# Cross-attention scores in a decoder layer: two one-pass matmuls over 128 rows instead of one fp32 matmul over 64, and the weighing of values in two halves

## The chip, the cores and the metric

The kernel runs on one core of a Trainium2 chip, as one program. The metric is device time in microseconds (us) from start to end of an execution; lower is better. TensorE is called PE here, its weight loads PEld, VectorE DVE, ScalarE ACT, GpSimd POOL, SyncE SP.

## The reference, cut to what matters

A decoder layer on x of shape (4, 512, 512): self-attention with 16 heads of 128 channels, cross-attention with 8 heads, and a feed-forward part whose weights are rounded to three values. The change lies in the cross-attention.

```python
x = x + attn(layernorm(x), Wq, bq, Wk, bk, Wv, bv, Wo, bo)   # 16 heads, attention between channels
x = x + xattn(layernorm(x), ctx, ctx, gamma)
x = x + ffn(layernorm(x), w1, w3, w2)                        # silu(x w1') * (x w3'), then w2'; hidden size 1365

def xattn(q, k, v, gamma):            # k and v are both ctx
    B, Dq, Lq = q.shape               # 4, 512, 512
    qh = q.reshape(B, 8, 64, 512)     # a head is 64 whole rows
    kh = k.reshape(B, 8, 64, 512)
    vh = v.reshape(B, 8, 64, 512)
    qk = einsum('bhdq,bhdl->bhql', qh, kh) / sqrt(64)
    sm = softmax(qk, axis=-1)
    ret = einsum('bhql,bhdl->bhdq', sm, vh)
    return gamma * ret.reshape(B, 512, 512)
```

So each head's scores are a 512 x 512 matrix that sums over only 64 rows, and the result sums over 512 keys into 64 rows.

## The kernel before, in words

**Two kinds of matmul.** An fp32 matmul leaves two records in the profile, a matmul on operands of type F32R one ("one-pass"). F32R holds fewer digits, so the kernel cuts an operand into a high part, rounded to F32R, and a remainder (`h` and `l`), and `products` (lines L311 to L336) adds up matmuls of such parts: L318 for the high parts, L319 for the remainders, L330 for a third part. Names with `_1h` are its results, as in `pu_1h`; `uh`, `ul`, `ud` are parts of a left operand, `ol` and `xl` of another, `fxh` and `fxl` of the feed-forward input.

**Order of the work.** Image b=0's self-attention comes first, with weights as they arrive; it leaves cut weights in DRAM. Then a loop over b = 1, 2, 3 runs the self-attention of image b on PE, four groups of heads each (`u`, `y`, `m`, scores `sc`, output `po`). Beside it two generators are stepped: `side` does `row_norms(b - 1)` and then `cross(b - 1)`, `quant` rounds the feed-forward weights. `products` calls `tick()` three times per pair of its results; the class `Side` (L163) takes as many steps of its generator at each tick as keep it in proportion: `CROSS_STEPS + NORM_STEPS` steps over `TICKS + 6` ticks. The last image's cross-attention runs in the same way beside the feed-forward matmuls `h` (L1005) and `y` (L1032) of the first images; in that part DVE makes `gf`, `gl` and the row statistics of the next feed-forward input. Within these ticks the program is put in order by a scheduler from the order of issue and from what is ready; each engine then works strictly in its order.

**The cross-attention.** A block c is 128 rows: two heads of 64. There are four blocks per image, 16 in all.

- `row_norms` (L638) takes mean and 1/std of each row of the self-attention's result `acc`, stores them to DRAM (`norm_a`, L648, issued on POOL) and loads them back in another layout (`norms`, L650, on POOL): one column pair per block. `settle` (L569) is a small DVE instruction on the loaded tile.
- `prepare(c)` loads the 128 rows of x (`cx`), normalizes them on DVE (`qs`, L117), loads `keys`, and transposes these on PE into `vals`. All of its loads are issued on POOL.
- `softmax_rows(c, m)` (L673) takes 128 queries of both heads: one fp32 matmul per head over 64 rows (`xs`, L680), the two heads in different rows of the array, then maxima on DVE (L686), exponentials on ACT (L692), the scaling by 1/sum on DVE (L704).
- `transpose_rows(c, m)` transposes the weights on PE (`xp`, L123) and DVE and ACT copy them to `pt`.
- `weigh_values(c)` (L717) runs after four such steps: eight fp32 matmuls of 128 x 64 by 128 x 512 (`xo`, L724), two heads in different columns of the array, then gamma and the addition of x on DVE (L731) and the store of `x_c`.

The steps are woven: transposition follows two softmax steps behind, the values of c are weighed during the first step of c+1, and block c+1 is prepared after step m = 2 of block c. Pools have three buffers for `cx`, two for `qs`, `keys`, `vals` and `pt`, four for `p`. POOL also issues the loads and stores of the rounded weights and adds the bias to `acc`; the SP queue brings the attention's weights.

## Time and profile before

| | |
|---|---|
| median of 3 runs | 1184.07 us (1180.95 to 1184.69) |
| the profiled execution | 1185.08 us, its span 1183.3 us |
| granted clock of PE, mean | 0.999 |
| `xs` L680, 256 records | 72.0 us busy on PE |
| `xo` L724, 256 records | 61.7 us busy on PE |
| `xp` L123, 512 records | 65.7 us busy on PE |
| maxima L686, 128 on DVE | 83.9 us |
| exponentials L692, 128 on ACT | 87.1 us |
| DMA | 254.11 MB, mean 215 GB/s |

The span is from the first to the last instruction; the time of an execution has some 2 us around it. Busy times of PE overlap, since matmuls are pipelined: the mean duration of a record is longer than the distance from one start to the next, and only the latter says what a matmul takes of the span. Records are counted, not calls: an fp32 matmul leaves two. PE's busy time by stage, from windows of the trace: 65.39 of the first 75 us, 195.31 of the 200 us to 275, 199.04 of the 200 to 475, 224.69 of the 225 to 700, and 478.49 of the 483 after it. The chain that ended last runs over PE for 80% of the span.

In the rows of the page an operation is given as out<-in by the program's names, then partitions x elements; "x256" is the number of records. A timeline row is start, duration, engine, line, operation. Windows list for each stretch its length, busy time of PE, PEld, DVE, ACT and POOL, the granted clock (1.00 is full), the DMA engines' busy share and GB/s.

### The profile page before, as it was taken

How to read it: one execution, taken by the hardware profiler on the slowest of the kernel's cores; microseconds unless marked ns; L12 is line 12 of the kernel's file. 1: busy time of each engine (PE TensorE's matmuls, PEld its weight loads, DVE VectorE, ACT ScalarE, POOL GpSimd, SP SyncE). 2: the span in 40 equal slices, each digit the busy share in tenths (PEclk: the TensorE clock that was granted, in tenths of full speed). 3: DMA queues.
4: the chain of work that ended last, by engine and by line, in shares of the span. 5: the costliest groups of instructions: out<-in, count | busy, mean ns of one | idle time of the engine just before them, and what ended most of it. 6: DMA issues, size and time to landing. Idle time of an engine off the chain costs nothing.

```text
span 1183.3 us, 16165 instructions
## 1 busy us (share of the span) xinstructions
PE 1162.9 (98%) x5278; PEld 821.8 (69%) x5278; DVE 805.7 (68%) x1806; ACT 452.0 (38%) x948; POOL 247.6 (21%) x419
## 2 busy tenths in 40 slices
PE   7999999999999999999999999999999999999998
PEld 3476674777767667777676677777667767768886
DVE  5879678978687966767587758586866745535232
ACT  2221223434434433434254424343454746634020
POOL 3545343431121223001111320011011000000000
PEclk9999999999999999999999999999999999999999
DMA  9898996786788659776876597587772220011201
GB/s 311 275 354 314 329 362 221 269 308 230 234 272 299 188 209 330 252 245 231 284 272 234 185 346 255 175 323 257 292 244 83 72 72 10 18 63 45 71 1 54
DMA packets 140030, 254.11 MB, mean 215 GB/s; under 512 B 16164, under 2 KB 47188, under 8 KB 139946
## 3 DMA queue, kind: packets, MB, share of 16 engines
q1 hardware_dynamic: 112266, 164.93, 41.4%
q0 software_dynamic: 27680, 88.16, 20.7%
q8 instruction: 42, 0.69, 0.2%
q14 instruction: 42, 0.34, 0.1%
HBM read 190.09 MB, written 62.93 MB: 214 GB/s over the span
## 4 chain that ended last, share of the span: by engine, by line
PE 80%; DMA 7%; DVE 6%; issue 3%; POOL 1%; ACT 1%; SPq 0%; DVEq 0%; POOLq 0%; ACTq 0%
PE h L1005 14%; PE y L1032 7%; PE xs L680 6%; PE xo L724 5%; PE xp L123 4%; PE sc L488 4%; PE po L525 4%; PE pg L409 2%; PE py_3h L318 1%; PE pu_1d L330 1%; PE py_3h L319 1%; PE py_1h L318 1%; DMA v_raw<-in_wv_dram 1%; PE pu_3d L330 1%; PE py_3d L330 1%
## 5 line engine op out<-in xcount | busy, mean ns | idle before, releaser
L1005 PE MATMUL h<-fxh,t 128*128 128x512 f32 (+1 forms) x352 | 139.8, 397 | 0.0
L692 ACT ACTIVATE p<-xs,xnmax 128x512 f32<-128x512 f32 x128 | 87.1, 688 | 135.7 <-PE xp L123 117.8
L1005 PE MATMUL h<-fxl,t 128*128 128x512 f32 (+1 forms) x352 | 137.4, 390 | 0.0
L686 DVE TENSOR_REDUCE xnmax<-xs 128x1 f32<-128x512 f32 x128 | 83.9, 682 | 18.1 <-PE xs L680 18.1
L1005 PEld LDWEIGHTS h<-fxh,t 128*128 128x128 f32 (+1 forms) x352 | 65.0, 185 | 18.4 <-issue 1.9
L1005 PEld LDWEIGHTS h<-fxl,t 128*128 128x128 f32 (+1 forms) x352 | 65.0, 185 | 14.6 <-issue 0.2
L680 PE MATMUL xs<-keys,qs 64*128 64x512 f32 x256 | 72.0, 640 | 0.0
L1032 PE MATMUL y<-t,gh 128*128 128x512 f32 (+1 forms) x176 | 69.6, 396 | 0.0
L1032 PE MATMUL y<-t,gl 128*128 128x512 f32 (+1 forms) x176 | 68.8, 391 | 0.0
L123 PE MATMUL xp<-ident,p 128*128 128x128 f32 x512 | 65.7, 272 | 0.0
L123 PEld LDWEIGHTS xp<-ident,p 128*128 128x128 f32 x512 | 59.0, 140 | 9.5 <-issue 2.3
L1016 DVE SCALAR_TENSOR_TENSOR gf<-h,scales_w,sl 128x512 f32<-128x512 f32 (+1 forms) x44 | 32.8, 746 | 46.1 <-PE h L1005 37.9
L724 PE MATMUL xo<-pt,vals 128*64 128x512 f32 x256 | 61.7, 599 | 0.9 <-ACT pt L126 0.9
L126 ACT COPY pt<-xp 128x512 f32<-128x512 f32 x96 | 53.5, 595 | 17.9 <-PE xp L123 17.9
L704 DVE TENSOR_SCALAR p<-p,xrden 128x512 f32<-128x512 f32 x128 | 57.5, 492 | 3.4
L525 PE MATMUL po<-m,eT 128*128 128x512 f32 x128 | 58.8, 601 | 0.1
L352 PE MATMUL pm<-u,v_raw 128*128 128x512 f32 x128 | 55.6, 592 | 0.0
L623 POOL DMA_DIRECT2D t_w<-tern_w x43 | 28.8, 672 | 119.9 <-DVE tern_w L616 47.9
L1014 ACT ACTIVATE sl<-h,scales_w 128x512 f32<-128x512 f32 (+1 forms) x44 | 30.1, 689 | 59.1 <-PE h L1005 58.9
L135 POOL CAST gh<-gf 128x512 fp32r<-128x512 f32 (+1 forms) x24 | 14.8, 617 | 177.0 <-DVE gf L1016 156.3
L527 DVE SCALAR_TENSOR_TENSOR acc<-po,acc 128x512 f32<-128x512 f32 x64 | 41.6, 681 | 7.5 <-PE po L525 7.4
L488 PEld LDWEIGHTS sc<-y,q 128*128 128x128 f32 x384 | 44.0, 192 | 2.5 <-issue 2.3
(299 smaller groups left out, 2667.7 us busy)
## 6 DMA issues: line engine op xcount, KB each, us to landing
oh<-kept_oh SPq DMA_DIRECT2D x48, 256.0 KB, 4.6
ol<-kept_ol SPq DMA_DIRECT2D x48, 256.0 KB, 4.9
kh<-kept_kh SPq DMA_DIRECT2D x48, 256.0 KB, 4.8
kl<-kept_kl SPq DMA_DIRECT2D x48, 256.0 KB, 5.2
vh<-kept_vh SPq DMA_DIRECT2D x48, 256.0 KB, 5.7
vl<-kept_vl SPq DMA_DIRECT2D x48, 256.0 KB, 6.1
q<-kept_q SPq DMA_DIRECT2D x48, 256.0 KB, 5.5
od<-kept_od SPq DMA_DIRECT2D x44, 256.0 KB, 5.9
```

Source lines behind the costliest of these rows:

```text
L123: nc.tensor.transpose(pt[:, ts(k, P)], src[:, ts(k, P)], ident)
L126: nc.scalar.copy(dst, pv)
L352: nc.tensor.matmul(p, lhsT=lhs(k)[:, ts(i, P)], rhs=rhs(k), start=(k == 0), stop=(k == 3))
L488: nc.tensor.matmul(sc[:, ts(g, DH)], lhsT=w[k][:, ts(g, DH)], rhs=ys[k][:, ts(g, DH)], start=(k == 0), stop=(k == KC - 1),)
L525: nc.tensor.matmul(po, lhsT=eT[:, g, :], rhs=ms[g], start=True, stop=True)
L680: nc.tensor.matmul(sc, lhsT=qs[rows, ts(m, P)], rhs=keys[rows, :], start=True, stop=True)
L686: nc.vector.reduce_max(nmax[:, j : j + 1], scs[j], axis=AX.X)
L692: nc.scalar.activation(p, scs[j], AF.Exp, bias=nmax[:, j : j + 1], scale=xscale, accum_out=den[:, j : j + 1],)
L704: nc.vector.tensor_scalar(ps[j], ps[j], rden[:, j : j + 1], None, ALU.mult)
L724: nc.tensor.matmul(po[rows, :], lhsT=vals[:, l, rows], rhs=pt[j][:, l, :], start=(l == 0), stop=(l == NC - 1),)
L1005: nc.tensor.matmul(ph[:r, :], lhsT=t[:, block(i, k)], rhs=fxT[j][:, k, :], start=(k == 0 and j == 0), stop=(k == KC - 1 and j == 1),)
L1032: nc.tensor.matmul(py, lhsT=g[i][j][:r, ts(c, P)], rhs=t2[:r, i, :], start=(i == 0 and j == 0), stop=(i == NHC - 1 and j == 1),)
```

## The change

**Scores.** Each head gets a left operand of 128 rows: the normalized queries' high part in rows 0 to 63 and their remainder in rows 64 to 127. The keys' high part stands in both halves of a second tile (`kh`), their remainder in both halves of a third (`kl`). Two one-pass matmuls, [qh; ql] with [kh; kh] and with [kl; kl], add up in one PSUM bank. To get this, `fetch(c)` loads each head's x rows and key rows twice, one copy above the other, in 64-row transfers on POOL; `split(c)` then issues per head, in this order, a normalization in place on ACT, a copy to F32R on ACT, a subtraction on DVE for the lower half, a copy of the keys on ACT, and their subtraction on DVE. The tiles of a head have two buffers, for the two heads of a block.

**Norms.** They are stored as -mean/std and 1/std and loaded twice, once into each half of the partitions, one column pair per head.

**Values.** `weigh_values(c, h)` runs for each two transposed steps, on 256 queries, so `pt` tiles are half as wide, and twice as many groups of matmuls `xo` and of additions run. The rows of x for the addition are loaded once per block at h == 0. `keys` and `vals` have one buffer and are prepared later, `cx` has one.

**Steps.** `CROSS_STEPS` goes from 40 to 49: preparation is three steps (values and fetch after m = 2, split after m = 3), and weighing comes twice per block. A small tile (`gate`) gets four buffers.

```diff
@@ -216,7 +216,7 @@
     def gate_of(src):
 
 
-        gate = small.tile([P, 3], F32, tag="gate", name="gate")
+        gate = small.tile([P, 3], F32, tag="gate", bufs=4, name="gate")
         for i, f in enumerate((H_OF / S, -1.0)):
             nc.vector.tensor_scalar(gate[:, i : i + 1], src[:, 0:1], f, f, ALU.max, ALU.min)
         nc.vector.tensor_tensor(gate[:, 2:3], gate[:, 1:2], ident[:, P - 1 :], ALU.add)
@@ -631,8 +631,9 @@
 
 
     xscale = 1.0 / math.sqrt(XD)
-    CROSS_STEPS = NC * (2 * NC + 2)
+    CROSS_STEPS = 3 * NC * NC + 1
     NORM_STEPS = 2 * NG + 3
+    HALF = T // 2
     norms = {}
 
     def row_norms(b, accs):
@@ -644,42 +645,75 @@
             yield
             moments(mv[:, g, :], accs[g], f"c_{b}_{g}")
         rstd = rstd_of(mv, f"c_{b}")
-        nc.vector.tensor_copy(mv[:, :, 1:2].rearrange("p c s -> p (c s)"), rstd)
+        mean, var = (mv[:, :, i : i + 1].rearrange("p c s -> p (c s)") for i in range(2))
+        nc.vector.scalar_tensor_tensor(mean, mean, -1.0, rstd, ALU.mult, ALU.mult)
+        nc.vector.tensor_copy(var, rstd)
         nc.gpsimd.dma_start(norm_a[b].rearrange("(p g) s -> p g s", g=NG), mv)
-        norms[b] = small.tile([P, NC, 2], F32, tag="norms", bufs=2, name=f"norms_{b}")
-        nc.gpsimd.dma_start(norms[b], norm_a[b].rearrange("(c p) s -> p c s", p=P))
+        norms[b] = small.tile([P, 2 * NC, 2], F32, tag="norms", bufs=2, name=f"norms_{b}")
+        for half in (slice(0, XD), slice(XD, P)):
+            nc.gpsimd.dma_start(norms[b][half], norm_a[b].rearrange("(n p) s -> p n s", p=XD))
         for _ in range(3):
             yield
 
     def cross(b, cx, cin, cpp, cpt):
+
 
 
         def load(dst, src):
             nc.gpsimd.dma_start(dst, src)
             return dst
 
-        def prepare(c):
-
-            xc = load(cx.tile([P, D], F32, tag="x", name=f"cx_{b}_{c}"), x_a[b][ts(c, P), :])
-            qs = cin.tile([P, D], F32, tag="qs", name=f"qs_{b}_{c}")
-            normalize(qs, xc, norms[b][:, c, 0:1], norms[b][:, c, 1:2])
-            keys = load(
-                cin.tile([P, T], F32, tag="keys", name=f"keys_{b}_{c}"), kv[b][ts(c, P), :]
+        def twice(tile, rows):
+            for half in (slice(0, XD), slice(XD, P)):
+                load(tile[half, :], rows)
+            return tile
+
+        def heads_of(c):
+            return [slice(c * P + j * XD, c * P + (j + 1) * XD) for j in range(2)]
+
+        def fetch(c):
+
+            raw[c] = [
+                [
+                    twice(cin.tile([P, T], F32, tag=f"{n}d", bufs=2, name=f"{n}d_{b}_{c}_{j}"), src[r, :])
+                    for n, src in (("x", x_a[b]), ("k", kv[b]))
+                ]
+                for j, r in enumerate(heads_of(c))
+            ]
+
+        def split(c):
+            halves[c] = []
+            for j, (xd, kd) in enumerate(raw.pop(c)):
+                n = 2 * c + j
+                nc.scalar.activation(
+                    xd, xd, AF.Identity, bias=norms[b][:, n, 0:1], scale=norms[b][:, n, 1:2]
+                )
+                q = cin.tile([P, T], F32R, tag="qs", bufs=2, name=f"qs_{b}_{c}_{j}")
+                nc.scalar.copy(q, xd)
+                low = slice(XD, P)
+                nc.vector.tensor_tensor(q[low, :], xd[low, :], q[low, :].bitcast(F32), ALU.subtract)
+                kh = cin.tile([P, T], F32R, tag="kh", bufs=2, name=f"kh_{b}_{c}_{j}")
+                nc.scalar.copy(kh, kd)
+                kl = cin.tile([P, T], F32R, tag="kl", bufs=2, name=f"kl_{b}_{c}_{j}")
+                nc.vector.tensor_tensor(kl, kd, kh.bitcast(F32), ALU.subtract)
+                halves[c].append((q, kh, kl))
+
+        def fetch_keys(c):
+            keys[c] = load(
+                cin.tile([P, T], F32, tag="keys", bufs=1, name=f"keys_{b}_{c}"), kv[b][ts(c, P), :]
             )
-            vals = cin.tile([P, NC, P], F32, tag="vals", name=f"vals_{b}_{c}")
-            transpose_blocks(vals, keys, f"vt_{b}_{c}", c % 2)
-            return xc, qs, keys, vals
+
+        def values(c):
+            vals[c] = cin.tile([P, NC, P], F32, tag="vals", bufs=1, name=f"vals_{b}_{c}")
+            transpose_blocks(vals[c], keys.pop(c), f"vt_{b}_{c}", c % 2)
 
         def softmax_rows(c, m):
 
-            _, qs, keys, _ = inputs[c]
             scs = []
-            for j in range(2):
+            for j, (q, kh, kl) in enumerate(halves[c]):
                 sc = bank(f"xs_{b}_{c}_{m}_{j}")
-                rows = slice(j * XD, (j + 1) * XD)
-                nc.tensor.matmul(
-                    sc, lhsT=qs[rows, ts(m, P)], rhs=keys[rows, :], start=True, stop=True
-                )
+                nc.tensor.matmul(sc, lhsT=q[:, ts(m, P)], rhs=kh, start=True, stop=False)
+                nc.tensor.matmul(sc, lhsT=q[:, ts(m, P)], rhs=kl, start=False, stop=True)
                 scs.append(sc)
             nmax = small.tile([P, 2], F32, tag="xnmax", name=f"xnmax_{b}_{c}_{m}")
             for j in range(2):
@@ -705,58 +739,72 @@
             return ps
 
         def transpose_rows(c, m, ps):
-            if m == 0:
-                pts[c] = [
-                    cpt.tile([P, NC, T], F32, tag="pt", name=f"pt_{b}_{c}_{j}") for j in range(2)
+            h = m // 2
+            if m % 2 == 0:
+                pts[c, h] = [
+                    cpt.tile([P, NC, HALF], F32, tag="pt", name=f"pt_{b}_{c}_{h}_{j}")
+                    for j in range(2)
                 ]
             for j in range(2):
                 transpose_blocks(
-                    pts[c][j][:, :, ts(m, P)], ps[j], f"xp_{b}_{c}_{m}_{j}", j or m % 2
+                    pts[c, h][j][:, :, ts(m % 2, P)], ps[j], f"xp_{b}_{c}_{m}_{j}", j or m % 2
                 )
 
-        def weigh_values(c):
-            xc, _, _, vals = inputs.pop(c)
-            pt = pts.pop(c)
-            po = bank(f"xo_{b}_{c}")
+        def weigh_values(c, h):
+
+            if h == 0:
+                xcs[c] = load(cx.tile([P, D], F32, tag="x", name=f"cx_{b}_{c}"), x_a[b][ts(c, P), :])
+            pt = pts.pop((c, h))
+            po = bank(f"xo_{b}_{c}_{h}")[:, :HALF]
             for l in range(NC):
                 for j in range(2):
                     rows = slice(j * XD, (j + 1) * XD)
                     nc.tensor.matmul(
                         po[rows, :],
-                        lhsT=vals[:, l, rows],
+                        lhsT=vals[c][:, l, rows],
                         rhs=pt[j][:, l, :],
                         start=(l == 0),
                         stop=(l == NC - 1),
                     )
+            xc = xcs[c][:, ts(h, HALF)]
             nc.vector.scalar_tensor_tensor(xc, po, gam, xc, ALU.mult, ALU.add)
-            load(x_c[b][ts(c, P), :], xc)
-
-        inputs, pts, rows = {}, {}, {}
+            if h == 1:
+                load(x_c[b][ts(c, P), :], xcs.pop(c))
+
+        raw, halves, keys, vals, pts, rows, xcs = {}, {}, {}, {}, {}, {}, {}
+        fetch(0)
+        fetch_keys(0)
         settle(norms[b][:, 0, :])
-        inputs[0] = prepare(0)
+        yield
+        split(0)
         yield
         order = [(c, m) for c in range(NC) for m in range(NC)]
         due = None
-        for i in range(len(order) + 2):
+        for i in range(len(order) + 3):
             if i < len(order):
                 c, m = order[i]
                 rows[c, m] = softmax_rows(c, m)
                 yield
             if due is not None:
-                weigh_values(due)
+                weigh_values(*due)
                 due = None
                 yield
-            if i < len(order) and m == 2 and c + 1 < NC:
-                inputs[c + 1] = prepare(c + 1)
+            if i < len(order):
+                if m == 2:
+                    values(c)
+                    if c + 1 < NC:
+                        fetch(c + 1)
+                        fetch_keys(c + 1)
+                    yield
+                if m == 3 and c + 1 < NC:
+                    split(c + 1)
+                    yield
+            if 2 <= i < len(order) + 2:
+                tc_, tm = order[i - 2]
+                transpose_rows(tc_, tm, rows.pop((tc_, tm)))
                 yield
-            if i >= 2:
-                c, m = order[i - 2]
-                transpose_rows(c, m, rows.pop((c, m)))
-                yield
-                if m == NC - 1:
-                    due = c
-        weigh_values(due)
-        yield
+                if tm % 2:
+                    due = tc_, tm // 2
 
 
     TICKS = HG * 3 * 6
@@ -891,7 +939,7 @@
     quant = Side(quantize(), QUANTIZE_STEPS, (B - 1) * TICKS)
     cpool = [
         cpools.enter_context(tc.tile_pool(name=n, bufs=k, side="right"))
-        for n, k in (("c_x", 3), ("c_in", 2), ("c_p", 4), ("c_pt", 2))
+        for n, k in (("c_x", 1), ("c_in", 2), ("c_p", 4), ("c_pt", 2))
     ]
     wpools = ExitStack()
     wp, stp = (
```

## The prediction

> **What bounds the kernel now.** I read the page's busy shares first, then TensorE's timeline around the score matmuls, then the places where TensorE stands still, and last the queues that would have to deliver the new operands. In the first fence the reader is to see that TensorE (PE) is busy for nearly the whole span. In the second, that this is not padding: one-pass matmuls over 128 rows follow each other every 0.23 us, and the gaps open only at `xs` (scores) and `xo` (weighed values).
>
> ```profile
> span 1183.3 us, 16165 instructions
> PE 1162.9 (98%) x5278; PEld 821.8 (69%) x5278; DVE 805.7 (68%) x1806; ACT 452.0 (38%) x948; POOL 247.6 (21%) x419
> ```
>
> ```profile
> 704.39 0.39 PE L319 MATMUL pu_1h<-ol,xl 128*128 128x512 f32 x1
> 704.71 1.13 PE L680 MATMUL xs<-keys,qs 64*128 64x512 f32 x4
> 705.76 0.50 PE L318 MATMUL pu_1h<-oh,xh 128*128 128x512 f32 x1
> 706.10 0.39 PE L319 MATMUL pu_1h<-ol,xl 128*128 128x512 f32 x1
> 706.33 0.40 PE L318 MATMUL pu_1h<-oh,xh 128*128 128x512 f32 x1
> ...
> 308.03 0.39 PE L319 MATMUL pu_2h<-ol,xl 128*128 128x512 f32 x1
> 308.35 3.65 PE L724 MATMUL xo<-pt,vals 128*64 128x512 f32 x16
> 311.93 0.50 PE L318 MATMUL pu_2h<-oh,xh 128*128 128x512 f32 x1
> 312.27 0.40 PE L319 MATMUL pu_2h<-ol,xl 128*128 128x512 f32 x1
> 312.50 0.39 PE L318 MATMUL pu_2h<-oh,xh 128*128 128x512 f32 x1
> ```
>
> So from about 245 us to the end what is saved on PE is saved in full, and any time for which PE waits is lost in full.
>
> **What is saved at the scores.** Starts count, since durations overlap. The step into an `xs` pair is 0.32 us (704.39 to 704.71), the pair takes 1.05, the step after it 0.34, and then steps are 0.23 again. 0.32 + 1.05 + 0.34 less two ordinary steps is 1.25 us for one pair of heads. The other pairs in the timeline repeat it. The changed kernel runs four one-pass matmuls over 128 rows, the shape of `pu_1h`: 4 x 0.227 = 0.91, with no odd step around them. There are 64 pairs (256 records, two for one fp32 matmul, two heads): 64 x 0.34 = 21.8 us less.
>
> A rule of the Trainium skill speaks against this. "TensorE: Matmul & The Clock Gate", section "Measured speedup vs the span model", says that tiles packed into the array cost one matmul's duration plus about 4 ns for each further tile. By it the two heads, packed by rows, would take two records of 0.43 us and hardly more, 0.86, and four one-pass matmuls at 0.91 would be 0.05 dearer: +3 us in all instead of -21.8. The row decides: 1.25 us with its surroundings, every time. What I pay less for is entering and leaving the packed form, not passes.
>
> **What the halved values cost.** `xo` is packed too, by columns: 0.32 + 3.58 + 0.34 - 0.46 = 3.78 us for 16 records in 8 simultaneous pairs. With e for the end of a packed block and s for a step, 2s + e = 1.05 (`xs`) and 8s + e = 3.58 give s = 0.42, e = 0.21. A half keeps the eight steps at half the columns: 8 x 0.21 + 0.21 + 0.20 (odd steps around it) = 2.1; two are 4.2 against 3.78, so +0.41 x 16 = +6.6 us. No row shows a packed matmul of 256 columns. Lower bound: +0.35 x 16 = +5.6 (only the second entry and exit). Upper: the weight loads of the two tiles, 137 ns each in the next fence, no longer fit beneath a step of 0.21 and run one after the other, s = 0.27: 8 x 0.06 x 32 = +15 more. I take +6.6, as in `sc` 128-column fp32 records with loads of 192 ns still start about 0.11 apart (249.56 to 253.04 for 32), so loads overlap. PE alone: -21.8 + 6.6 = -15.2 us.
>
> **What ScalarE, VectorE and POOL get.**
>
> ```profile
> L187 DVE TENSOR_TENSOR ul<-u,uh x48: 671/683/693, 222.1 to 832.0; 128x512 fp32r<-128x512 f32 x48
> L186 ACT ACTIVATE uh<-u 128x512 fp32r<-128x512 f32 x48 | 30.3, 632 | 39.5 <-DVE u L340 38.8 <-DMA acc<-in_x_dram 0.7
> L117 DVE TENSOR_SCALAR qs<-cx,norms x16: 530/538/548, 244.9 to 972.1; 128x512 f32<-128x512 f32 x16
> L724 PEld LDWEIGHTS xo<-pt,vals x256: 132/137/137, 308.3 to 1062.5; 128*64 128x64 f32 x128
> ```
>
> Per block of keys (16 in all) ACT gets two normalizations and four copies: 96 x 0.63 = 60 us, 38% becomes 43%. DVE gets four subtractions, 64 x 0.683 = 44, loses 16 x 0.538 = 8.6, and splits one 0.75 us addition into two of some 0.45 (between 0.28 for 128 columns and 0.75 for 512: +2): +37 us, 68% becomes 71%, and near 79% in the image loop. POOL issues 128 more half-height loads at 0.54 us (69 us) and four more loads of the norms at 0.76; the bytes are 128 x 128 KB = 17 MB on 254. All this lies beside PE, which is the bound; uncovered it costs only where PE finds an operand unready. The transfers have a whole block (about 45 us) for landings of about 5 us. The SP queue, which brings the weights, keeps its order.
>
> **Where a new wait comes.** Queries, key halves and remainders have two buffers for two heads, so those of block c+1 can't be written until the last `xs` of c is read. From the order in which the changed program's instructions stand: in the image loop PE has 8 to 10 us of other matmuls in between; at 0 to 1 DVE has two maxima (1.36), one sum, two `ul` and two `ud` (3.4), and the four subtractions (2.7), with a small one 7.7 us against PE's 9.9. That fits. In the feed-forward part at block 0 to 1 PE has 8.6 us (32 `h` matmuls and 12 transposes), but DVE stands at two maxima 1.4, scalings of `p` 2.0, `fxl`, `gf`, `gl` 2.1, four row statistics of 0.66 with aggregates 3.0, subtractions and small ones 1.9 before the first remainder is done: 10.4, a wait of 1.6, and some 0.9 more for the second head: +2.5 us. Behind it on PE's queue stand the `y` matmuls.
>
> The other place is the first `xs` of an image. The fence shows the norms' way through DRAM for the first one.
>
> ```profile
> 224.72 0.55 POOL L648 DMA_DIRECT2D norm_a<-mv_c  x1 [1.68 <-DVE mv_c L647]
> 231.40 0.76 POOL L650 DMA_DIRECT2D norms<-norm_a  x1 [6.13 <-DMA norm_a<-mv_c]
> ...
> 243.20 0.16 DVE L573 TENSOR_TENSOR norms<-norms,one 128x1 f32<-128x1 f32 x1
> ...
> 247.06 0.40 PE L319 MATMUL pm_0h<-ul,vl 128*128 128x512 f32 x1
> ...
> 255.05 1.13 PE L680 MATMUL xs<-keys,qs 64*128 64x512 f32 x4
> ```
>
> Before, `xs` comes at 255.05, long after the norms. In the changed order it stands right behind that `pm_0h`, at 247.3, while on DVE the two instructions that finish the norms have moved behind the `y` sums (which end near 235.2). So the store goes out at 236.3, the two loads stand behind it and behind three additions of `acc` on POOL; with the store's 6.4 us they go at 242.7 and 243.5, and with the load's 4.1 us the second lands at 247.6. Then ACT (two normalizations, a copy) and DVE (a piece's sum, two `m` sums, a subtraction) need some 2.7 us: 250.3, a wait of 3.0. Behind ACT's waiting instruction are the copies of `pm_0t`, behind DVE's settling of the norms the `m` sums. The second image's norms go out at 450 as before and fit by 0.7 us; the third has the same order.
>
> The second rule: "DMA: Bandwidth & Descriptors", section "Anatomy of one DMA — SWDGE (gpsimd) path", gives a transfer about 2.0 us of fixed cost. By it the second load would land at 244.2 and PE would wait for nothing. Here the rows read 6.4 and 4.1, so I take the wait. Such a wait can also cost clock:
>
> ```profile
> 71.70:74.90 3.20, 0.46 (x3) 0.06 (x1) 1.62 (x5) 2.90 (x10) 2.06 (x4) 1.00 1.07 395
> 75.00:78.30 3.30, 3.30 (x8) 2.58 (x9) 2.56 (x7) 1.82 (x4) 2.23 (x4) 0.50 1.04 399
> 162.40:165.00 2.60, 0.39 (x3) 0.04 (x1) 1.61 (x5) 1.59 (x9) 1.82 (x4) 1.00 1.05 407
> 165.00:168.00 3.00, 3.00 (x13) 2.46 (x14) 2.96 (x9) 1.96 (x4) 2.21 (x5) 1.00 1.07 399
> ```
>
> After PE stood idle to 74.84 the granted clock was 0.50 for about 3.4 us (1.7 us lost); after the shorter pause at 162 it stayed 1.00. A wait of 3.0 lies between: I count +4.0 for wait and clock (bounds 0 and +6.7).
>
> **Sum.** -21.8 + 6.6 + 2.5 + 4.0 = -8.7 us. The profiled execution took 1185.08 (span 1183.3 and 1.8 around it), so 1176.4; it stands 1.0 over the median of 1184.07: about 1175.5.
>
> **Rivals.** (B) No new wait: the queues absorb both. Then -15.2: 1169. For it: ACT has room and DVE waits for no transfer in the image loop. Against: the norms' two landings are measured. (C) Halved values expose their weight loads: +15 on the sum, 1191, or 1184 with no wait. For it: 137 ns twice is more than 0.21. Against: the tiles' loads start together, and `sc`. (D) The other side: the halves come late at every block, at the first `xs` of all 16 groups. For it: single-height buffering, DVE near 79%, and DVE itself waits (31 times for exponentials, 37.6 us in all), while ACT and DVE serve strictly in order. At 2 us a group +32 takes the place of the 6.5: 1184.07 - 15.2 + 32 = 1201. It decides from 1.0 us a group, where the saving is gone. Against: PE's 8 to 10 us of other work. (E) That the change doesn't do what it says is unlikely: the order shows 256 score matmuls over 128 rows in place of 128 over 64.
>
> **Numbers.** 0.3% (3.6 us: 1180.5 to 1187.6) is about what a measurement can tell from no change. The likeliest case 0.55 (its own range 1169 to 1182), B 0.15, C 0.10, D 0.20. Faster: 0.50 + 0.15 + 0.01 = 0.66; same: 0.05 + 0.04 + 0.04 = 0.13; slower 0.21. The range reaches from B's lower edge, 1167, into D, to 1194.
>
> **What would show it.** Right: `xs` steps of 0.23 us with the neighbours at 0.23 too; `xo` blocks of about 1.9 us, 32 of them; PE idle for 2 to 5 us before the first `xs` near 247, waiting for DVE `qs`; a wait of 2 to 3 us in the feed-forward part; other matmuls as before. Wrong: `xo` steps of 0.27; waits for `kl` or `qs` before every first `xs`; a DVE wait for staged weight pieces; PE below full clock away from 250 us.

## The result, and the profile after

The changed kernel takes 1194.41 us (median of 4 runs, 1193.77 to 1195.95) against 1184.38 of before beside it: ratio 1.0086, 95% interval 1.0066 to 1.0107. It is slower by some 10 us, where 8.7 us less were forecast.

On PE the change did what it was to do. Two timeline pieces of the changed kernel (start, duration, engine, line, operation):

```profile
250.32 0.39 PE L319 MATMUL pm_0h<-ul,vl 128*128 128x512 f32 x1
250.55 0.39 PE L715 MATMUL xs<-kh,qs 128*128 128x512 f32 x1
250.77 0.39 PE L716 MATMUL xs<-kl,qs 128*128 128x512 f32 x1
251.00 0.39 PE L715 MATMUL xs<-kh,qs 128*128 128x512 f32 x1
251.23 0.39 PE L716 MATMUL xs<-kl,qs 128*128 128x512 f32 x1
251.45 0.62 PE L330 MATMUL pm_0d<-ud,vd 128*128 128x512 f32 x2
...
332.83 0.39 PE L330 MATMUL py_2d<-kd,gd 128*128 128x512 f32 x1
333.15 1.95 PE L762 MATMUL xo<-pt,vals 128*64 128x256 f32 x16
335.03 0.50 PE L318 MATMUL py_2h<-kh,gh 128*128 128x512 f32 x1
335.37 0.40 PE L319 MATMUL py_2h<-kl,gl 128*128 128x512 f32 x1
```

Four score matmuls take 0.90 us (250.55 to 251.45) with ordinary steps on both sides; the pair of before took 1.25 with its surroundings. A half of the values takes 0.32 + 1.88 + 0.34 less two ordinary steps, 2.08, so two take 4.16 against 3.78: +0.38 a block, 6.1 us in all, of which the prediction had 6.6. The gain was lost elsewhere, in waits. The page's first lines:

```profile
span 1192.0 us, 17122 instructions
PE 1155.2 (97%) x5534; PEld 871.5 (73%) x5534; DVE 838.5 (70%) x1874; ACT 503.7 (42%) x1041; POOL 320.5 (27%) x551
```

And from PE's list of waits between 213 and 884 us, the images beside which the cross-attention runs (waiting operation, what it waited for: us in all, times, longest):

```profile
PE pu_1d L330 <- ACT e L501: 3.2, 2, 1.6
PE py_0d L330 <- DMA kd<-kept_kd: 2.1, 4, 1.2
PE pm_0d L330 <- DVE vd L304: 1.9, 2, 1.4
PE xo L762 <- ACT pt L126: 1.9, 3, 1.3
PE pu_3d L330 <- DMA od<-kept_od: 1.5, 2, 1.1
```

PE is busy 7.7 us less than before and the span is 8.7 longer, so PE stands 16.4 us more. No entry of this list is at scores: PE waits there only in the feed-forward part (2.5 us in all). In the images PE waits at matmuls of the self-attention and at `xo`, 14.9 us in all by the list against 2.3 before; the list names ACT first, but no single entry is large.

Because the first 200 us, which hold none of the change, differ from one profiled execution to the next (image 1's first matmul started anywhere from 208.2 to 218.0 us), I compare two later stretches of the traces: the image loop, from image 1's first `pu` to the first `h`, and the feed-forward part, from there to the end. Each kernel has one trace. Kernels that run the same program in a stretch differ in it by up to 3 us, so smaller differences in the two right columns say nothing.

| kernel | median us | ratio to before, 95% | image loop us | feed-forward us |
|---|---|---|---|---|
| before | 1184.38 | | 667.7 | 301.7 |
| changed | 1194.41 | 1.0086 (1.0066 to 1.0107) | 671.6 | 307.1 |
| e1 | 1187.99 | 1.0030 (1.0014 to 1.0045) | 659.2 | 313.3 |
| e2 | 1187.55 | 1.0016 (1.0004 to 1.0027) | 672.5 | 302.7 |
| e3 | 1243.10 | 1.0472 (1.0432 to 1.0512) | 724.9 | 302.8 |
| e4 | 1193.73 | 1.0064 (1.0041 to 1.0087) | 672.6 | 306.8 |
| e5 | 1183.87 | 0.9974 (0.9961 to 0.9987) | 662.6 | 305.8 |
| e6 | 1212.88 | 1.0240 (1.0208 to 1.0272) | 696.0 | 302.8 |
| e7 | 1181.89 | 0.9972 (0.9959 to 0.9986) | 660.8 | 305.9 |
| e8 | 1184.21 | 0.9987 (0.9973 to 1.0001) | 662.4 | 308.4 |
| e9 | 1207.87 | 1.0179 (1.0155 to 1.0203) | 686.6 | 307.4 |
| e10 | 1187.31 | 1.0010 (0.9997 to 1.0023) | 659.4 | 310.3 |
| e11 | 1214.97 | 1.0236 (1.0210 to 1.0262) | 684.8 | 314.0 |
| e12 | 1180.17 | 0.9953 (0.9936 to 0.9970) | 659.2 | 305.8 |
| e13 | 1182.93 | 0.9970 (0.9956 to 0.9984) | 661.4 | 307.3 |
| e14 | 1181.77 | 0.9959 (0.9938 to 0.9981) | 660.5 | 305.6 |

The runs of before beside the experiments had medians of 1185.5 to 1186.7; the ratios are each to the runs of before on the same chip.

**Following one wait.** PE's wait at 714 us, in image 3's stage, shows the chain. First PE, then POOL, ACT and DVE, all of the changed kernel:

```profile
713.89 0.39 PE L330 MATMUL pu_1d<-od,xd 128*128 128x512 f32 x1
715.93 1.43 PE L330 MATMUL pu_1d<-od,xd 128*128 128x512 f32 x5 [1.65 <-ACT e L501]
```

```profile
701.52 2.08 POOL L663 DMA_DIRECT2D xd<-x_a  x4 [0.70 <-DVE qs L694]
...
708.78 0.81 ACT L688 ACTIVATE xd<-xd,norms 128x512 f32<-128x512 f32 x1 [5.81 <-DMA xd<-x_a]
709.61 1.28 ACT L726 ACT_TABLE_LOAD   x1
710.91 0.69 ACT L726 ACTIVATE p<-xs,xnmax 128x512 f32<-128x512 f32 x1
...
712.25 0.81 ACT L688 ACTIVATE xd<-xd,norms 128x512 f32<-128x512 f32 x1
714.37 0.37 ACT L501 ACTIVATE e<-sc,nmax 128x128 f32<-128x128 f32 x1 [1.31 <-DVE nmax L497]
```

```profile
712.39 0.17 DVE L736 RECIPROCAL xrden<-xden 128x2 f32<-128x2 f32 x1 [6.26 <-ACT p L726]
712.59 0.88 DVE L738 TENSOR_SCALAR p<-p,xrden 128x512 f32<-128x512 f32 x2
713.38 0.69 DVE L496 TENSOR_REDUCE nmax<-sc 128x4 f32<-128x512 f32 x1
```

The `xd` of block 1 is loaded from 701.52 on, when block 0's splitting has let its buffers go. After two copies ACT comes to that block's normalization, which is needed only a block later, and ACT stands for 5.81 us until the transfer has landed. Behind it are the exponentials `p` of the running block; DVE's reciprocal of their sums waits 6.26 us for them, and behind it on DVE are the maxima `nmax` of the self-attention's scores. So its exponentials `e` come late, and PE, which waits for them at `pu_1d` (with a matmul that doesn't read `e`; presumably it needs the PSUM bank from which `e` is made), stands 1.65 us. ACT's entries for this instruction in the list of waits of the whole run (4.7 of the 46.1 us are in the feed-forward part):

```profile
ACT xd L688 <- DMA xd<-x_a: 46.1, 18, 5.8
...
ACT xd L688 <- DMA norms<-norm_a: 17.5, 3, 7.5
```

### The profile page after: what moved, and what is told of

It reads as the page before. It is cut to its first block, busy times and chain, and to the rows that moved or that the text cites. A ratio compares the mean times of both kernels' runs of the same rounds, so it can differ in the third digit from the quotient of the medians.

```text
span 1192.0 us, 17122 instructions
## 1 busy us (share of the span) xinstructions
PE 1155.2 (97%) x5534; PEld 871.5 (73%) x5534; DVE 838.5 (70%) x1874; ACT 503.7 (42%) x1041; POOL 320.5 (27%) x551
## 5 line engine op out<-in xcount | busy, mean ns | idle before, releaser
L762 PE MATMUL xo<-pt,vals 128*64 128x256 f32 x512 | 64.8, 386 | 4.2 <-ACT pt L126 3.4
L762 PEld LDWEIGHTS xo<-pt,vals 128*64 128x64 f32 x512 | 34.6, 136 | 29.8 <-issue 9.5
L688 ACT ACTIVATE xd<-xd,norms 128x512 f32<-128x512 f32 x32 | 25.7, 813 | 68.0 <-DMA xd<-x_a 46.1
L715 PE MATMUL xs<-kh,qs 128*128 128x512 f32 x128 | 51.0, 398 | 1.2 <-DVE fxl L136 0.8
```

The costliest lines, as they stand in the source:

```text
L715: nc.tensor.matmul(sc, lhsT=q[:, ts(m, P)], rhs=kh, start=True, stop=False)
L762: nc.tensor.matmul(po[rows, :], lhsT=vals[c][:, l, rows], rhs=pt[j][:, l, :], start=(l == 0), stop=(l == NC - 1),)
```

## The experiments

Theory A: ACT works in order, and an instruction that was put right behind its load holds all that stands behind it. Theory B: the added bytes and issues slow the weights. Theory C, the prediction's rival D: the halves come late because of their single-height buffers.

**e1: the normalizations where they are issued.**

```diff
-                nc.scalar.activation(xd, xd, AF.Identity, bias=..., scale=...)
+                tc.keep_in_program_order(nc.scalar.activation(xd, xd, AF.Identity, bias=..., scale=...))
```

> The changed kernel, with one thing different: the 32 normalizations on ACT are held behind what the program issued on ACT before them, where the scheduler had put those of block c+1 up to some 16 places ahead, right behind their loads. Theory A (ACT stands for the loads of the next block's queries, 46.1 us over 18 times, and the exponentials of the running block, the self-attention's e and the evictions of PSUM wait behind it): ACT's waits for xd fall below 10 us, PE's waits for ACT e at pu_1d and pu_3d (6 us) go, as do most at xo for pt; 6 to 9 us less, 1186 to 1188. Theory B (the 17 MB more of loads and the 128 more issues slow the weights' transfers): no change beyond 1 us. Theory C (single buffering of q, kh, kl: DVE's subtractions come late): the wait at the first xs of a block grows, since the chain starts later: slower, 1197 or more.

Ratio 1.0030 where the change had 1.0086, about 6.6 us less. In the image loop the gain is larger, 12.4 us (659.2 against 671.6), and it puts this stretch 8.5 us under before. ACT's wait for `xd` from DMA, 46.1 us, is gone from the list, and so are PE's waits of 1.60 and 1.65 us for `e` near 490 and 714. That is what theory A expects. PE's longest waits between 213 and 872 us in e1:

```profile
PE py_0d L330 <- DMA kd<-kept_kd: 2.5, 6, 0.9
PE xo L762 <- ACT pt L126: 1.9, 3, 1.3
PE pm_0d L330 <- DVE vd L304: 1.8, 2, 1.3
```

The waits for `e`, for the weights `od` and some small ones for DVE are gone, 7.2 us in all. Of the other 5, 1.7 are a stretch of half clock that the changed kernel's trace has near 245 us and e1's has not (e5's has it again, so it is not the edit's); the rest stands in no entry of the lists. In the feed-forward part 6.2 us more are lost: here e1's entry in PE's list of waits, and one of the four in the timeline:

```profile
PE xs L715 <- DVE qs L694: 6.8, 4, 3.5
```

```profile
921.43 0.39 PE L1053 MATMUL h<-fxl,t 128*85 128x512 f32 x1
923.99 0.50 PE L715 MATMUL xs<-kh,qs 128*128 128x512 f32 x1 [2.17 <-DVE qs L694]
```

So, held back, the chain normalization, copy, subtraction is hidden where PE has other matmuls, and bare where it has few. The place is the one that theory C names, but not its reason: at the wait shown the scores of the block before had ended near 913 us, and ACT came to the normalizations only at 921.2, behind exponentials and copies. No run gave the halves more buffers.

**e2: before, with only the values in halves.**

```diff
-            po = bank(f"xo_{b}_{c}")
+            po = bank(f"xo_{b}_{c}_{h}")[:, : T // 2]
...
-                if m == NC - 1:
-                    due = c
+                if m % 2:
+                    due = c, m // 2
```

> The kernel before, with only the weighing of values in two halves of 256 queries (pt half as wide); scores as before. By the prediction's step +6.6 us on PE; from the blocks of the changed kernel's trace (1.88 us and 0.19 of odd steps around it, twice, against 3.78) +5.6. So 1190 if PE is simply longer and nothing else moves, ratio 1.005. If earlier weighing shortens a wait at xo for pt, less, 1187; if halving costs buffers (a pt half that is still read), more, 1193.

The two stretches add up to 975.2 us against 969.4: +5.8, close to the 6.1 of PE's blocks. The timed ratio says less, 0.5 to 3.2 us. The first 208 us of the profiled run were 5.7 faster than in the run of before, though nothing of the change runs in them; whether this kernel gains there regularly was not tested. The weighing is thus no cause of the loss beyond its own size.

**e3 and e6: before with halved values, and the change's loads into tiles that nobody reads.**

```diff
+                    extra = cin.tile([P, T], F32, tag=f"{n}d", bufs=2, ...)
+                    for half in (slice(0, XD), slice(XD, P)):
+                        load(extra[half, :], src[r, :])
```

> As the run before it, and with the eight loads of 64 rows per block that the changed kernel makes (queries and keys of each head twice), into tiles that nobody reads, on POOL. Theory B (bytes and issues slow the weights): 5 us or more over the run without these loads, with waits of PE for od, kd or other weights. Theory A: under 1.5 us over it, since no engine waits for these loads.

Measured: 56 us over e2 by the medians, in the letter what B expects (5 us or more), but far more than the same loads cost in the changed kernel. POOL's timeline tells why:

```profile
288.74 1.04 POOL L658 DMA_DIRECT2D kd<-in_kv_dram  x2 [3.43 <-DMA kd<-in_kv_dram]
292.21 1.04 POOL L658 DMA_DIRECT2D kd<-in_kv_dram  x2 [2.43 <-DMA kd<-in_kv_dram]
```

Since nobody waits for these loads, they had been put far ahead on POOL, each waiting for the one before it, and the loads that are needed stood behind them (DVE waited 17.2 us for `cx`). The run does not separate B from A. e6 holds each of these loads in its place (`tc.keep_in_program_order` around the `dma_start`).

> As the third experiment (the kernel before with halved values, and eight more loads of 64 rows per block into tiles that nobody reads), but each of these loads held behind what the program issued on POOL before it; in the third experiment all of them had been ordered far ahead, each waiting for the one before it in the same tile. Theory B (bytes and issues themselves slow the weights): 5 us or more over the second experiment, 1193. Theory A: under 2 us over it, 1188 to 1190; then the 55 us of the third experiment came from the place of the loads on POOL's queue.

Still 25 us over e2, so theory B has something in it. But the loss stands in three places only, at the start of each image: by the milestones of the two traces PE falls back by 7 us in image 1's first group, by 10 in image 2's, by 7 in image 3's, and by nothing between. PE's waits there are for weights:

```profile
PE py_0d L330 <- DMA kd<-kept_kd: 4.6, 5, 1.2
PE pm_0h L319 <- DMA vl<-kept_vl: 2.2, 2, 1.3
```

There the DMA engines are full anyway (a share of 1.03 to 1.08 between 460 and 480 us), and e6 brings two blocks' extra loads at once. In the changed kernel the second block's `xd` must wait for the first block's splitting (476.9 us in image 2) and the keys' loads came earlier; its waits for weights (`kd` 2.1, `od` 1.5) are 3.6 us in the image loop, against 0.5 before. So B is a price at the start of an image, some 3 us in the changed kernel by these waits; that it is small there because of the buffers that theory C blames is my reading and was not tested.

**e4: the normalizations on DVE.** The edit replaces `nc.scalar.activation` by `nc.vector.tensor_scalar` with the same factors.

> The changed kernel with the 32 normalizations of queries on DVE instead of ACT, not held back. Theory A in its narrow form (ACT alone is the trouble): ACT's wait for xd goes and PE gets 5 us or more back: 1187 to 1189. In its wider form (any engine that works in order is held when such an instruction stands ahead of its load): DVE waits for xd instead, and since DVE has every maximum, sum and remainder behind it, no gain or a loss: 1193 to 1200. Theory B: no change beyond 1 us.

```profile
DVE xd L688 <- DMA xd<-x_a: 25.2, 9, 6.1
DVE xd L688 <- DMA norms<-norm_a: 15.1, 3, 7.7
```

The wait moved to DVE, with the longest as long as on ACT, and the image loop stayed at 672.6 us. So it is not ACT's load that matters (ACT has 23 us less to do here) but the place of the instruction behind its transfer, on whichever engine.

**e5: held back in the images only.** `if b < B - 1:` ahead of the holding.

> As the first experiment, but the normalizations are held back only beside the three images' self-attention; beside the feed-forward part they stand where the changed kernel has them. Theory A with its bound (holding back pays where PE has other work for the 8 to 10 us that the chain of normalization, copy, subtraction takes, and costs where ACT is full): by the milestones of the traces PE reaches the feed-forward part 9 us ahead of before, as in the first experiment, and loses there 5 us as in the changed kernel, not 11: 4 us faster than before, ratio 0.997. If the loss in the feed-forward part has nothing to do with the holding back: as the first experiment, ratio 1.003.

Ratio 0.9974, as expected: faster than before by 1.5 to 4.6 us. Image loop 662.6, feed-forward part 305.8; over the eight kernels that hold back and leave the steps of the images where they are (e1, e5, e7, e8, e10, e12, e13, e14) the image loop takes 659.2 to 662.6, mean 660.7, that is 11 us under the changed kernel.

**e7, e10, e14: the feed-forward part.**

e7, the keys' copies on POOL there:

```diff
-                nc.scalar.copy(kh, kd)
+                (nc.scalar.copy if b < B - 1 else nc.gpsimd.tensor_copy)(kh, kd)
```

> As the fifth, and beside the feed-forward part the keys' copies to F32R (two per block) run on POOL instead of ACT. In the changed kernel's trace ACT was busy 9.91 of the 10 us from 930 on, with five table loads of 1.28 us, and PE stood 1.7 and 0.6 us for the remainders of the keys. If ACT is what makes the halves late there: 2 to 3.5 us less than the fifth, ratio 0.995. If DVE is (it has the row statistics and maxima before the subtraction, by the prediction's count 10.4 us against 8.6): within 1 us of the fifth, or slower, since POOL's copies come between its casts of gf.

305.9 against 305.8 us: nothing that the traces can tell. e10, four empty steps behind each splitting (`for _ in range(ROOM + 1 if b == B - 1 else 1): yield`, and the steps counted):

> As the fifth, and beside the feed-forward part there are four empty steps behind each splitting of the next block, so that 48, 48 and 64 matmuls of the feed-forward part (11 to 15 us) stand between the last scores of a block and the first of the next, instead of 32, 32 and 16. Prediction's own reading (the chain behind the last scores, 10.4 us by its count for the first block, is longer than PE's work there): the waits for kl, qs at the first scores of a block (2.5 us with the half clock behind it 4) go, the feed-forward part takes 302 to 303 us instead of 305.8; ratio 0.994 to 0.995. If another engine's lateness makes them (exponentials behind ACT's table loads): they turn up at xo or xp, no gain.

310.3 us, 4.5 more. The waits for `kl` and `qs` went down to 0.3, and others came, the second outcome. Waits of PE from 880 to 960 us:

```profile
PE xo L765 <- ACT pt L126: 3.2, 1, 3.2
PE xt_f L936 <- ACT sl L1066: 1.8, 1, 1.8
```

e14, normalizations and keys' copies both on POOL there:

> As the fifth, and beside the feed-forward part both the normalizations and the keys' copies run on POOL, so that ACT keeps only the copies of queries. ACT was busy 19.39 of 20 us in the changed kernel's stretch from 920 to 940 (16.91 before), and in the tenth run waits turned up for exponentials, sl and gh instead of kl. If ACT is the limit there: feed-forward part 302.5 to 304 us, ratio 0.995. If DVE's order is (maxima, sums, statistics ahead of the subtractions): 305 to 306, 0.997, and PE still waits for kl or qs from DVE.

305.6 us, with a wait of 1.8 for `qs` from DVE: by the number the second outcome. But ACT was not freed where it counts. The feed-forward part begins 11.9 us earlier in e14 than in the changed kernel and 3.4 earlier in before, so these three stretches hold the same part of the work to within 0.4 us (length, busy PE, PEld, DVE, ACT, POOL, clock, DMA share, GB/s), of the changed kernel, of e14 and of before:

```profile
920.00:940.00 20.00, 18.25 (x88) 14.04 (x87) 18.18 (x39) 19.39 (x34) 5.21 (x9) 0.95 0.32 96
```

```profile
908.00:928.00 20.00, 18.20 (x85) 14.21 (x84) 18.98 (x41) 18.28 (x30) 9.22 (x14) 0.93 0.40 119
```

```profile
917.00:937.00 20.00, 20.00 (x99) 14.76 (x98) 15.80 (x37) 18.18 (x30) 1.77 (x3) 1.00 0.21 66
```

In e14 ACT is still busy 18.28 of 20 us there, about as much as before, where PE works through. So ACT's load alone doesn't make the wait, but its order may share in it: in e14 the second copy of queries stands behind a table load and the exponentials on ACT, and then its subtraction behind `gl` and the scaling of `p` on DVE. Which of the two queues decides was not tested.

**e8, e9, e13: the norms.** e8 gives the norms' last steps a higher priority (`with tc.high_priority(400)` around the reciprocal, the product, the copy and the store):

> As the fifth, and the last steps of the rows' norms (reciprocal, product, copy on DVE, and the store) are given a higher priority, so that they stand right behind the statistics of the last row group, as in the kernel before, and not behind the y sums. In the changed kernel's trace the two loads of the norms then fell between POOL's additions to acc, and PE waited for vd: 0.9 and 1.6 us and some 1.7 of half clock, against 0.9 before. If the late norms make this: 3 us less than the fifth, ratio 0.995. If the wait for vd comes from the additions on POOL alone, which stay: within 1 us of the fifth.

No gain. The store went out at 224.36 us instead of 235.22, and a normalization of block 0 then stood ahead of the y sums' copies, waiting for the same norms:

```profile
235.99 0.82 ACT L692 ACTIVATE xd<-xd,norms 128x512 f32<-128x512 f32 x1 [8.04 <-DMA norms<-norm_a]
236.71 1.05 ACT L326 COPY py_0t<-py_0h 128x512 f32<-128x512 f32 x2
...
240.89 0.73 PE L331 MATMUL pm_0d<-ud,vd 128*128 128x512 f32 x2 [3.15 <-DVE vd L305]
```

e9 issues the two normalizations of a block one behind the other, and block 0's four steps later:

> As the eighth, but block 0's two normalizations of each image are issued four steps later and one right behind the other, so that on ACT they stand behind the copies of the stage's y and m sums instead of ahead of them. In the eighth run's trace ACT stood for the norms' load ahead of the copies of py_0t, the y sums came 3 us late, and PE waited 3.2 us for vd. Theory A (it is again ACT's place behind a landing that costs): the wait for vd at the first image shrinks to the 0.9 of before, no half clock near 240; the image loop, 662 us in the fifth and eighth, takes 658 to 659; ratio 0.994 to 0.995. If the additions on POOL alone slow vd: no change against the fifth, 0.997.

The wait for `vd` did go down to 0.5 us, and the kernel became 24 us slower than e5, which nobody expected. The steps' places had moved by four, so that the first scores of blocks 0 and 3 of every image (counted from 0; the expectation of e13 names blocks 1 and 3, the trace has 0 and 3) came close behind their block's normalizations:

```profile
257.69 1.75 PE L331 MATMUL pu_1d<-od,xd 128*128 128x512 f32 x7
262.36 0.50 PE L723 MATMUL xs<-kh,qs 128*128 128x512 f32 x1 [2.93 <-DVE qs L702]
...
258.89 1.55 ACT L693 ACTIVATE xd<-xd,norms 128x512 f32<-128x512 f32 x2
```

One of the six windows of ten microseconds (the clock is the third number from the end):

```profile
260.00:270.00 10.00, 7.64 (x26) 5.92 (x27) 8.30 (x17) 4.51 (x11) 2.62 (x5) 0.83 0.73 231
```

Six times a wait of about 2.8 us and a clock of 0.83 over 10 us (1.7 us lost): 6 x 4.5 = 27, less some 3 won at the start against e8, the 24 us of the image loop. This is the bare chain of e1's feed-forward part again. At 262 and at 382 us ACT began the block's normalizations 3.5 us before the scores, and PE was ready 2.9 and 2.8 us before them. Buffers are not what made it late: block 0 has no block ahead of it, and the scores ahead of block 3 had ended 9 us before. e9 also puts the second normalization of every block ahead of the first head's copy, so the shift was not tried by itself; blocks 1 and 2 had the pair too and no wait. e11 put e9 and e10 together.

> The ninth and the tenth together: holding back in the images, early norms, later first splitting, room in the feed-forward part. If the two losses are independent, the sum: 6 to 7 us under the fifth, from image 1's first matmul to the end 961 to 962 us, against 969.4 before; ratio 0.991 to 0.992. PE's matmuls alone would give 969.4 - 16 = 953. If freed time only moves a wait elsewhere: 0.995 or more.

1.0236: both losses, 684.8 and 314.0 us.

**e12 and e13: the old scores beside the feed-forward part.** e12 is e5, with the last image's scores as one fp32 matmul of 64 rows per head and the normalization on DVE.

```diff
+            if b == B - 1:
+                xd, kd = halves[c] = raw.pop(c)
+                normalize(xd, xd, norms[b][:, c, 0:1], norms[b][:, c, 1:2])
+                return
...
+                    nc.tensor.matmul(sc, lhsT=xd[r, ts(m, P)], rhs=kd[r, :], start=True, stop=True)
```

> As the fifth, but the last image's cross-attention, which runs beside the feed-forward part, keeps the scores of before (one fp32 matmul of 64 rows per head, normalization on DVE), with values in halves. The second experiment's trace spent 302.7 us in the feed-forward part with just this, the fifth 305.8. If what is lost there comes from the halves' work on ACT and DVE: 302.5 to 303 us there, image loop as in the fifth (659 to 662), ratio 0.994 to 0.996. If it is lost to the coarser way in which the steps are woven: 305 and more, 0.997.

Ratio 0.9953, the lowest of all: 3.6 to 7.6 us under before, though the intervals of e5, e7, e13 and e14 overlap with it. But not for the reason given: the feed-forward part is again 305.8 us, as in e5, the second outcome. The wait for `kl` is gone, and so is what the new scores saved on PE; the sum is the same. Of the 3.1 us over e2, 1.6 are the last weighing behind its transposition, a matter of how the steps are woven:

```profile
1043.11 0.65 PE L786 MATMUL xo<-pt,vals 128*64 128x256 f32 x2 [1.58 <-ACT pt L126]
```

e13 adds e8's early norms, with block 0's normalizations in a row behind the copies:

> As the run before it, and in the images the norms' last steps have a higher priority, with block 0's second normalization right behind the first (in the eighth run it stood alone ahead of the copies of py_0t and held them; in the ninth four steps more had moved the first scores of blocks 1 and 3 to where PE had nothing else). Theory A: no ACT wait for norms ahead of py_0t, PE's wait for vd at the first image back to under 1 us and no half clock near 240: image loop 657 to 659 us, ratio 0.992 to 0.994. If the additions on POOL alone slow vd: as the run before it.

0.9970, image loop 661.4 instead of 659.2: nothing won. The norms' store went out at 229.13 us, no ACT wait stood ahead of the copies of `py_0t`, and PE still waits 2.28 us for `vd` and 2.0 for `kd` from DVE (1.1 in the changed kernel). So late norms alone are not the cause at the first image's start; what delays DVE there stays open between POOL's additions and DVE's own queue.

## Why the prediction was wrong

The terms of the prediction can be added up by stretch. For the image loop it forecast 7.4 us less than before (-16.3 for scores, +4.9 for halves, +4.0 for the first image's start); it came 3.9 more. For the feed-forward part it forecast 1.3 less; it came 5.4 more. With the normalizations held back the image loop comes 7.0 less, so there one missing term of 11 us makes nearly the whole difference, even if the waits that are left are not the ones that were forecast.

- *"`xs` steps of 0.23 us"*: right, 0.90 for four instead of 1.25. Rival B's full saving is on PE.
- *"+6.6 us"* for the halves: 6.1 from PE's blocks, +5.8 in e2's trace; the timed e2 says 0.5 to 3.2. Rival C's exposed weight loads did not occur: 1.88 is eight steps of 0.21 and an end of 0.2.
- *"uncovered it costs only where PE finds an operand unready"* and *"The transfers have a whole block (about 45 us) for landings of about 5 us"*: this is the step that failed. I had looked for PE's operands and for queues in front of them, and counted ACT's 60 us of work, not where ACT's instructions would stand. They stood right behind transfers that single buffers let start late; ACT stood 46.1 us for them, and what it held was other work. Holding them back (e1, e5) gave 11 us of the image loop back, and e4 showed that it is the place and not the engine. In the sum this term was zero. That the buffers make the loads late is read from one POOL row (701.52, released by a subtraction of block 0); no run gave these tiles more buffers.
- *"a wait of 3.0"* before the first `xs`, with clock +4.0: the size came out right by luck, the place and the cause were wrong. From image 1's first matmul to its first `sc`, PE fell 4.3 us behind before; but it waited for `vd`, not at `xs`, with the clock at 0.83 from 240 to 250. The norms' lateness, by which I had worked it out, is not the cause by itself (e8, e13).
- *"+2.5 us"* in the feed-forward part: right where it was worked out, too small for the stretch. At block 0 to 1 PE lost 1.7 and 0.6 us at 935 to 938, 2.3 in all. What it left out, by the steps of the timeline: 1.8 for half clock behind that wait, 0.9 at 918, and 1.6 at 1057, where PE waits for `pt` from ACT. Some 2.5 us of the 6.7 by which the stretch missed its forecast are not accounted for. Giving PE more work there (e10) only moved the wait.
- Rival D, *"the halves come late at every block"*: not in the changed kernel, where no first `xs` of the image loop waited; e9 made it at six of twelve groups, by the place of the chain and not by the buffers. Its reason, single-height buffering, came in by another door: the buffers let the loads start late, and the loads held ACT. That a step which isn't on PE's path can hold an engine for another's work was in none of the rivals.

What stays open: of the 12 us that PE's matmuls save in the image loop (48 pairs at 0.34 less 12 blocks at 0.38) the held-back kernels show 7 (660.7 against 667.7). Some of the rest is at the first image's start and in the weights' waits at the start of images 2 and 3; e6 bounds what extra loads can do there, no run takes them away. In the feed-forward part neither ACT's nor DVE's order was tried by itself.

## What to carry to other kernels

When a change gives an engine work that is not on the critical path, ask where each of these instructions will stand in the engine's order and what it waits for there: an instruction placed right behind its load, long before its result is needed, holds everything behind it on its engine until the load has landed (up to 5.8 us at a time here). Holding it back to where the program has it turned a loss of 10 us into a gain of 1.5 to 4.6, but only where the bound engine has enough other work to cover the chain behind it: the same hold cost 6 us in another stage. Four steps' shift of a woven side task, with two instructions exchanged, cost 24 us, so such a change is measured stage by stage, not as a whole.

## What the runs showed of the hardware

**VectorE and GpSimd.** DVE's `vd` sums take 0.74 us alone. While POOL added to `acc`, a sum took 2.62 and 2.71 in the changed kernel, with POOL's additions at their 1.29; in before three sums took 0.98, 1.77 and 1.78, and two of the additions 1.73 and 1.74. Rows of DVE and POOL, of before and then of the changed kernel:

```profile
237.99 5.03 DVE L304 SCALAR_TENSOR_TENSOR vd<-vl,one,vh 128x512 fp32r<-128x512 f32 x4
235.87 5.94 POOL L783 TENSOR_TENSOR acc<-acc,bo_bc 128x512 f32<-128x512 f32 x4 [0.50 <-DVE bo_bc L573]
```

```profile
238.10 6.57 DVE L304 SCALAR_TENSOR_TENSOR vd<-vl,one,vh 128x512 fp32r<-128x512 f32 x4
236.37 3.79 POOL L831 TENSOR_TENSOR acc<-acc,bo_bc 128x512 f32<-128x512 f32 x3
241.50 1.28 POOL L831 TENSOR_TENSOR acc<-acc,bo_bc 128x512 f32<-128x512 f32 x1
```

Four sums took 6.57 us instead of 5.03. The Trainium skill ("SBUF — State Buffer", section "SBUF: two separate sides") says of the port pair that the two engines share that, of a VectorE instruction with two SBUF inputs (as here) and a GpSimd one, whichever starts first has it for the whole instruction and the other "fully blocks". The first long sum (238.10 to 240.72) agrees if it waited for the rest of one addition and for a whole one behind it, so the loser can lose twice. The second (240.64 to 243.35) doesn't fit: the addition that it overlaps began 0.86 us after it, and until then POOL only issued the loads of the norms. What held it stays open.

**The clock.** In the changed kernel about 1.9 us of standing between 240 and 244 us, and 1.75 between 935 and 938, were each followed by some 3.4 us at half clock, while e1 stood about 1.75 at the same place near 240 and kept the full clock, as did the changed kernel after 1.6 us at 490. So pauses well under 3 us can cost 1.7 us more, but not each does.
